# Two edits to the attention of a fused sequence layer: an addition made by a product with the identity, and one pair moved behind the first convolution

## The chip, the cores and the metric

The kernel runs on one core of a Trainium2 chip. The core has TensorE (PE: matrix products from SBUF into PSUM), VectorE (DVE), ScalarE (ACT), GpSimd (POOL) and SyncE (SP), each with its own instruction stream; they meet through semaphores. TensorE's loading of weights appears in the profile as a row of its own (PEld). All data are fp32. The metric is the device time of one execution in microseconds (us); lower is better. Before the change it is 3857.62 us, the median of three runs (3856.37 to 3858.19).

## The reference

x has 4 batches, 512 time steps, 128 frequencies and 64 channels, so D = 8192 numbers a time step. Layer 0 computes, for each batch:

```
xn = layernorm(x)                          # over D
k, v, r = xn @ Wk, xn @ Wv, sigmoid(xn @ Wr)   # 64 numbers a step
s_t = decay * s_(t-1) + k_t * v_t          # a scan over time
x = x + (r * s) @ Wo                       # the attention
x = x + gelu(conv over frequency(layernorm(x)) + freq_b)
x = x + layernorm(depthwise conv over time(layernorm(x)) + time_b)
x = x + gelu(x @ W1 + b1) @ W2 + b2        # on the 64 channels
```

Layer 1 takes a moving average over time, and adds what a Fourier transform, a product for each channel, and the inverse transform make of the rest. The change touches only the attention and the convolution over frequency of layer 0.

## The kernel before

Layer 0 keeps time on the free axis: D is cut into 64 chunks of 128 rows, taken as 32 pairs of chunks, and a tile of a pair has 128 partitions and 2 x 512 numbers. Each batch goes through five stages: `project` (J) and `scan` (Z), `attend_and_convolve` (A), `convolve_time` (C), `open_feed` (O) and `feed_forward` (F). Two stages of different batches run side by side. `in_turn` steps two Python generators in turn, by the share that each `yield` states: batch 0's A beside batch 1's J; then batch 0's C beside batch 1's A; then batch 0's F beside batch 2's J, batch 1's C beside batch 2's A, batch 1's F beside batch 3's J, batch 2's C beside batch 3's A, and so on. A lead given for each stretch sets how far one side runs ahead.

The order of TensorE's instructions is the order in which these generators issue them. The other engines are ordered by the framework's scheduler, which also sets the semaphores; each engine then works its own list strictly in order. Transfers into SBUF are issued on SP's queue, stores on POOL's.

The stage that the change touches is A, from L466. For pair i it has three steps:

- `attend(i)`, L475: SP loads x of the pair (`xp`, three buffers) and a 128x128 piece of Wo (`wo_sb`). TensorE makes two products with 64 rows each (L482) into the PSUM tile `a`, which has two banks and one buffer, so a product waits until the one before has been read. VectorE adds x (L484), which gives `x1` in SBUF, and multiplies by the layer norm's factor of each time step (L488), which gives `z`.
- `convolve(i)`, L498: three groups of products, L503 (the norm's mean and the bias), L512 (the neighbouring chunks: pairs i-1 and i+1) and L517 (the chunk itself), into the tile `c` or `m`. ScalarE applies GELU in place (L518), VectorE adds `x1` (L520), which gives `x2`; POOL stores it, ScalarE squares it (L523), and scales the weights of pair i+2 (L496).
- `add_up(i)`, L250: TensorE sums x2 and its square over the rows into the tile `st`, for the next layer norm.

The loop at L533 issues `attend(i)`, `convolve(i - 2)`, `add_up(i - 3)`. The first convolution therefore follows the third `attend`, though it needs only pairs 0 and 1.

In C each pair costs VectorE two operations on 128x1024 (L556, L557) and four on 128x512 (L564), and ScalarE two activations (L560) and a square (L605); its column sums on TensorE go to the tile `p`. Batch 0's C makes all 32 pairs there; for batches 1 and 2, 12 of the 32 pairs have been made during an earlier F (`AHEAD`). When A begins, C's layer norm is not ready: its first step is the `finish` of the A before it (L262, L240), which stands on TensorE behind the first three convolutions of the A beside it.

Of the kernel before, what the change touches and what calls it, by code (L numbers as in the profile page):

```python
# [10 lines left out]
F32 = mybir.dt.float32  # L11
AF = mybir.ActivationFunctionType
ALU = mybir.AluOpType
# [3 lines left out]
P = 128  # L17
# [5 lines left out]
SL = 512  # L23
NS = D // SL
NPR = NCH // 2
# [54 lines left out]
def layer0(ctx, tc, dram, x, xt, vecs, wkvr, wo, wdec, wconv, fbias, w1, fb1, w2, fb2, x4):  # L80
# [4 lines left out]
    nc = tc.nc  # L85
# [7 lines left out]
    fr = ctx.enter_context(tc.tile_pool(name="fr", bufs=3))  # L93
# [9 lines left out]
    def two(pool, tag):  # L103
        return pool.tile([P, 2, SL], F32, tag=tag, name=tag)


    ident = const.tile([P, P], F32, name="ident")
# [51 lines left out]
    def neighbours(q, c):  # L159

        return (c - 1, q), (c + 1, 1 - q)

    def rows_of(q, d):

        return 1 - q if d < 0 else q
# [79 lines left out]
    def add_up(st, i, pair, squares, first, last):  # L245

        for j in range(2):
            for k, src in ((0, pair), (1, squares)):
                q = 2 * j + k
                nc.tensor.matmul(  # L250
                    st[32 * q : 32 * q + 32, :], lhsT=ones, rhs=src[:, j, :],
                    start=first, stop=last,
                )

    def finish(st, bank, tag):

        s_sb = rowp.tile([P, SL], F32, tag="s", name="s_sb")
        nc.scalar.copy(s_sb, st)
        yield CHAIN
        pm = bank()  # L260
        for t in range(NT):
            nc.tensor.matmul(  # L262
                pm[:, 2 * t : 2 * t + 2], lhsT=s_sb[:, t * P : (t + 1) * P], rhs=pick,
                start=True, stop=True,
            )
        me = tiny.tile([P, NT, 2], F32, tag=f"me{tag}", name="me")
        nc.vector.tensor_copy(me.rearrange("p t k -> p (t k)"), pm[:, 0 : 2 * NT])
        return me[:, :, 0], me[:, :, 1]

    def moments(mean, square, tag):  # L270

        var, rs, mrs = cols(f"var{tag}"), cols(f"rs{tag}"), cols(f"mrs{tag}")
        nc.vector.tensor_tensor(var, mean, mean, ALU.mult)
        nc.vector.tensor_tensor(var, square, var, ALU.subtract)
        rsqrt(rs, var)
        nc.vector.tensor_tensor(mrs, mean, rs, ALU.mult)
        return rs, mrs

    def rows(bank, a, b, names):
        both = rowp.tile([P, 2, SL], F32, tag=names, name=names)  # L280
        for k, col in enumerate((a, b)):
            pb = bank()
            spread(pb, col)
            nc.scalar.copy(both[:, k, :], pb)
            yield CHAIN
        return both[:, 0, :], both[:, 1, :]

    def pair_of(row):
        return row.unsqueeze(1).to_broadcast([P, 2, SL])

    def load_x(b, i):
        xp = fr.tile([P, 2, SL], F32, tag="xp", name="xp")
        nc.sync.dma_start(xp, xt[b, 2 * i : 2 * i + 2].rearrange("c p t -> p c t"))
        return xp
# [4 lines left out]
    def c_bank():  # L299
        return two(ps_c, "c")  # L300
# [165 lines left out]
    def attend_and_convolve(b):  # L466
        rst, rs, mrs = scanned.pop(b)
        rb, mb = yield from rows(of_a, rs, mrs, "rm")

        nc.vector.tensor_scalar(mb, mb, at_one[:, 1:2], at_one[:, 0:1], ALU.mult, ALU.add)  # L470
        st = ps_s.tile([P, SL], F32, tag="s", name="st")
        free_s[0] = False
        x1s, zs, ws, waiting = {}, {}, {}, {}

        def attend(i):  # L475
            xp = load_x(b, i)
            wo_sb = fr.tile([P, P], F32, tag="wo", name="wo_sb")
            nc.sync.dma_start(wo_sb, wo[:, i, :])
            at = two(ps_a, "a")
            for j in range(2):  # L480
                js = slice(j * S, (j + 1) * S)
                nc.tensor.matmul(at[:, j, :], lhsT=wo_sb[js, :], rhs=rst[js, :], start=True, stop=True)  # L482
            x1 = x1s[i] = fr.tile([P, 2, SL], F32, tag="x1", name="x1")
            nc.vector.tensor_tensor(x1, at, xp, ALU.add)  # L484
            z = fr.tile([P, 2, SL], F32, tag="z", name="z", bufs=4)
            for j in range(2):
                zs[2 * i + j] = z[:, j, :]
            nc.vector.tensor_tensor(z, x1, pair_of(rb), ALU.mult)  # L488

        def scaled(i):  # L490

            wcs = fr.tile([P, 2, P + H], F32, tag="wcs", name="wcs")
            for j in range(2):
                c = 2 * i + j
                ws[c] = wcs[:, j, :]
                nc.scalar.mul(wcs[:, j, :], wc_sb[:, i % 2, :], vec[:, G2, c : c + 1])  # L496

        def convolve(i):  # L498
            cv = c_bank() if i % 2 or held[0] else two(ps_m, "m")
            for h in range(2):  # L500
                for j in range(2):
                    q = 32 * (2 * h + j)
                    nc.tensor.matmul(  # L503
                        cv[h * H : (h + 1) * H, j, :], lhsT=cgr[q : q + 2, i, :], rhs=mb[q : q + 2, :],
                        start=True, stop=False,
                    )
            for j in range(2):
                c = 2 * i + j
                for n, h in neighbours(i % 2, c):
                    if 0 <= n < NCH:  # L510
                        rs = halves[rows_of(n // 2 % 2, n - c)]
                        nc.tensor.matmul(  # L512
                            cv[halves[h], j, :], lhsT=ws[n][rs, P:], rhs=zs[n][rs, :], start=False, stop=False
                        )
            for j in range(2):
                c = 2 * i + j
                nc.tensor.matmul(cv[:, j, :], lhsT=ws[c][:, 0:P], rhs=zs[c], start=False, stop=True)  # L517
            nc.scalar.activation(cv, cv, AF.Gelu_apprx_tanh)  # L518
            x2 = two(bk, "x2")
            nc.vector.tensor_tensor(x2, cv, x1s.pop(i), ALU.add)  # L520
            nc.gpsimd.dma_start(x2d[b][2 * i : 2 * i + 2].rearrange("c p t -> p c t"), x2)
            sq2 = bk.tile([P, 2, SL], F32, tag="sq", name="sq2")
            nc.scalar.activation(sq2, x2, AF.Square)  # L523
            for c in (2 * i - 2, 2 * i - 1):
                zs.pop(c, None)
                ws.pop(c, None)
            if i + 2 < NPR:
                scaled(i + 2)
            waiting[i] = x2, sq2

        for i in range(2):
            scaled(i)
        for i in range(NPR + 3):  # L533
            if i < NPR:
                attend(i)
                yield 1.0
            if 1 < i < NPR + 2:
                convolve(i - 2)
                yield 5.0
            if i > 2:  # L540
                add_up(st, i - 3, *waiting.pop(i - 3), i == 3, i == NPR + 2)
                yield 1.0
        begin[attend_and_convolve], free_s[0] = b + 1, True
        mean3, sq3 = yield from finish(st, of_a, 3)
        carried[b] = moments(mean3, sq3, 3)
# [206 lines left out]
    def nothing(b):  # L752
        yield 1.0

    J, Z, A, C, O, F = project, scan, attend_and_convolve, convolve_time, open_feed, feed_forward
    begin[A] = 0
    needed = {A: scanned, C: carried, O: causal, F: opened}
# [317 lines left out]
```

## Time and profile before

| what | value |
|---|---|
| median of the runs | 3857.62 us |
| the profiled execution's own time | 3842.84 us |
| its span, first to last instruction | 3840.8 us |
| TensorE busy | 3619.7 us, 94% |
| VectorE busy | 2692.2 us, 70% |
| ScalarE busy | 1764.0 us, 46% |
| GpSimd busy | 504.2 us, 13% |
| mean granted clock of TensorE | 0.984 |
| L484, x1 = a + x | 128 times, 1219 ns |
| L488, z = x1 times the factor | 128 times, 1219 ns |
| first `wo` product of batches 0, 1, 2, 3 | 219.95, 510.49, 1250.37, 1939.74 us |
| last column sum into `st` of batches 1, 2 | 790.9, 1491.1 us |

A line of the trace in order of time has the start, the duration (both in us), engine, line of the kernel, operation, what it writes and reads with its shape, the number of instructions merged into it, and in brackets how long the engine was idle before it and whom it waited for. Matmuls are pipelined and their ends are modelled, so that TensorE's duration and busy time run ahead of what it gets done; the distance from start to start is the better measure. VectorE's instructions overlap by some 0.1 us as well.

### The profile page before, as it was taken

The page shows a single profiled execution, that of the slowest core. Times are in us where ns is not written, and L with a number is a line of the kernel's source. Part 1 is how long each engine was busy: PE and PEld are TensorE (multiplying, and loading weights), DVE is VectorE, ACT ScalarE, POOL GpSimd, SP SyncE. Part 2 cuts the span into 40 slices and gives each one's busy share as a digit, 9 for nine tenths or more (in the row PEclk, how much of TensorE's full clock was granted, in tenths as well). Part 3 has the DMA queues.
Part 4 walks back from the last instruction along what each step waited for, and adds up shares of the span by engine and source line. Part 5 has one row for each costly group of instructions (what it writes and reads, how often), then busy time and mean ns, then how long its engine had stood idle before and what let it go on. Part 6 is the DMA issues. An engine that isn't in the chain of part 4 may idle for free. (4 is left out here: it accounts for less than half of the span.)

```text
span 3840.8 us, 44890 instructions
## 1 busy us (share of the span) xinstructions
PE 3619.7 (94%) x15945; PEld 1342.6 (35%) x15945; DVE 2692.2 (70%) x3498; ACT 1764.0 (46%) x2491; POOL 504.2 (13%) x782
## 2 busy tenths in 40 slices
PE   9999999988999999899999989999989999999999
PEld 4433322233333223333322323333322753327533
DVE  4455669968656896865689799855559267893577
ACT  0023345645556564555656578867744210142100
POOL 0000012212000121110022121100012100121001
PEclk9999999999999999999999999999999999999999
DMA  9867657777765788777568677645559468994687
GB/s 312 273 216 244 222 195 253 257 246 272 256 227 185 234 276 265 252 255 235 193 232 277 215 243 260 219 154 175 186 190 284 141 212 293 306 311 160 197 292 269
DMA packets 428599, 910.71 MB, mean 237 GB/s; under 512 B 33688, under 2 KB 84056, under 8 KB 424280
## 3 DMA queue, kind: packets, MB, share of 16 engines
q1 hardware_dynamic: 350080, 634.55, 50.3%
q0 software_dynamic: 75776, 271.62, 20.1%
q8 instruction: 127, 2.08, 0.2%
q10 hardware_dynamic: 2520, 1.67, 0.2%
q14 instruction: 96, 0.79, 0.1%
HBM read 639.21 MB, written 268.50 MB: 236 GB/s over the span
## 5 line engine op out<-in xcount | busy, mean ns | idle before, releaser
L667 PE MATMUL pa<-mid,w_sb 128*64 128x512 f32 x2048 | 503.7, 613 | 70.1 <-DVE x4t L672 69.9
L660 ACT ACTIVATE mid<-m,fb_sb 128x1024 f32<-128x1024 f32 x256 | 284.7, 1112 | 243.4 <-PE m L656 243.0
L672 DVE SCALAR_TENSOR_TENSOR x4t<-pa,fb_sb,x 128x512 f32<-128x512 f32 x252 | 187.6, 745 | 208.2 <-PE pa L667 208.2
L656 PE MATMUL m<-x,w_sb 64*128 64x512 f32 x1008 | 291.6, 651 | 1.0 <-ACT mid L660 0.7
L660 ACT ACTIVATE mid<-c,fb_sb 128x1024 f32<-128x1024 f32 x256 | 283.2, 1106 | 1.6 <-PE c L656 1.6
L667 PEld LDWEIGHTS pa<-mid,w_sb 128*64 128x64 f32 x2048 | 125.8, 137 | 417.5 <-issue 221.1
L656 PE MATMUL c<-x,w_sb 64*128 64x512 f32 x1008 | 265.6, 600 | 5.0 <-ACT mid L660 4.9
L360 PE MATMUL a<-xp,wx 128*128 128x512 f32 x512 | 245.0, 605 | 6.2 <-DVE wx L357 5.5
L943 PE MATMUL b<-xin,avg_sb 128*128 128x512 f32 x512 | 230.8, 593 | 3.1 <-DVE xin L949 3.1
L920 ACT COPY two<-a 128x512 f32<-128x512 f32 x64 | 37.5, 586 | 423.9 <-PE a L915 423.9
L523 ACT ACTIVATE sq<-x 128x1024 f32<-128x1024 f32 x128 | 135.0, 1054 | 203.0 <-DVE x L520 203.0
L949 DVE TENSOR_TENSOR xin<-b,pm 128x512 f32<-128x512 f32 x256 | 159.0, 683 | 95.5 <-PE b L946 80.5
L564 DVE SCALAR_TENSOR_TENSOR to<-kd,vec,to 128x510 f32<-128x510 f32 (+1 forms) x288 | 210.5, 743 | 17.9 <-ACT to L560 16.2
L633 ACT ACTIVATE kd<-kd,vec 128x512 f32<-128x512 f32 x256 | 193.5, 809 | 7.2 <-DVE kd L625 7.2
L250 PE MATMUL st<-x,ones 128*32 128x512 f32 x512 | 174.3, 603 | 14.0 <-DVE x L520 13.8
L825 DVE COPY xf<-b 128x256 f32<-128x256 f32 x128 | 54.3, 424 | 188.4 <-PE b L889 187.8
L681 PEld LDWEIGHTS pt<-ident,x4t 128*128 128x128 f32 x1024 | 107.9, 141 | 210.3 <-ACT mid L660 155.0
L846 DVE TENSOR_TENSOR uv<-xin 128x1024 f32<-128x1024 f32 x128 | 155.2, 1228 | 35.2 <-DMA edge<-x 14.7
L344 DVE BATCH_NORM_STATS2 stt<-wx 128x6 f32<-128x512 f32 x174 | 113.0, 685 | 93.3 <-DMA wx<-in_x 92.8
L357 DVE TENSOR_SCALAR wx<-wx,vec 128x192 f32<-128x192 f32 x174 | 48.6, 316 | 184.7 <-DMA wx<-in_wkvr 167.6
L482 PE MATMUL a<-rst,wo_sb 64*128 64x512 f32 x512 | 147.6, 650 | 32.3 <-DVE x L484 30.0
L484 DVE TENSOR_TENSOR x<-a,xp 128x1024 f32<-128x1024 f32 x128 | 156.0, 1219 | 20.9 <-PE a L482 17.6
(239 smaller groups left out, 6649.0 us busy)
## 6 DMA issues: line engine op xcount, KB each, us to landing
xp<-in_xt SPq DMA_DIRECT2D x256, 512.0 KB
xin<-x SPq DMA_DIRECT2D x128, 1024.0 KB
kh<-to SPq DMA_DIRECT2D x152, 512.0 KB
x<-x POOLq DMA_DIRECT2D x128, 512.0 KB, 4.1
kx<-x SPq DMA_DIRECT2D x128, 512.0 KB
x<-ob POOLq DMA_DIRECT2D x64, 1024.0 KB, 6.6
out<-xin POOLq DMA_DIRECT2D x64, 1024.0 KB, 7.3
x<-x SPq DMA_DIRECT2D x96, 512.0 KB
```

Source lines behind the costliest of these rows:

```text
L250: nc.tensor.matmul(st[32 * q : 32 * q + 32, :], lhsT=ones, rhs=src[:, j, :], start=first, stop=last,)
L360: nc.tensor.matmul(pa[:, k, :], lhsT=wq[:, j, k * P : (k + 1) * P], rhs=xp[:, j, :], start=first and j == 0, stop=last and j == 1,)
L484: nc.vector.tensor_tensor(x1, at, xp, ALU.add)
L564: nc.vector.scalar_tensor_tensor(to[:, j, k:], xr[:, j, : SL - k], vec[:, w, c], to[:, j, k:], ALU.mult, ALU.add)
L633: tc.keep_in_program_order(nc.scalar.activation(d[:, j, :], d[:, j, :], AF.Identity, bias=vec[:, B4, c], scale=vec[:, G4, c]))
L656: nc.tensor.matmul(pm[:, h, :], lhsT=w1_sb[hs, m * P : (m + 1) * P], rhs=x3[hs, :], start=True, stop=True)
L660: nc.scalar.activation(mid, pm, AF.Gelu_apprx_tanh, bias=fb1_sb[:, m : m + 1])
L667: nc.tensor.matmul(pa[h * H : (h + 1) * H, :], lhsT=w2_sb[:, m, :], rhs=mid[:, h, :], start=(m == 0), stop=(m == 1),)
L672: nc.vector.scalar_tensor_tensor(x4t, pa, fb2_sb, x3s[c // 2][:, c % 2, :], ALU.add, ALU.add)
L846: nc.vector.tensor_tensor(t, xin[:, 0:2, :], xin[:, 2:4, :], op)
L943: nc.tensor.matmul(po[j], lhsT=avg_sb[:, j, :], rhs=xin[:, j, :], start=True, stop=False)
L949: nc.vector.tensor_tensor(by_n(xin[:, j, :]), by_n(po[j]), by_c(pm[j % 2][:, j // 2, :]), ALU.add)
```

## The change

Two edits, both in `attend_and_convolve`. In batch 1, for the odd pairs, TensorE adds x: behind the two products with Wo it makes two more into the same PSUM tile, with the identity as weights and `xp` as the moving operand. ScalarE then copies the sum to `x1`, and VectorE makes `z` from the PSUM tile, not from `x1`. In all four batches the third pair's `attend` is issued behind the first convolution, with its two loads, and the step that it had in the taking of turns is left out.

```diff
             at = two(ps_a, "a")
+
+            summed = b == 1 and i % 2 == 1
             for j in range(2):
                 js = slice(j * S, (j + 1) * S)
-                nc.tensor.matmul(at[:, j, :], lhsT=wo_sb[js, :], rhs=rst[js, :], start=True, stop=True)
-            x1 = x1s[i] = fr.tile([P, 2, SL], F32, tag="x1", name="x1")
-            nc.vector.tensor_tensor(x1, at, xp, ALU.add)
+                nc.tensor.matmul(at[:, j, :], lhsT=wo_sb[js, :], rhs=rst[js, :], start=True, stop=not summed)
+            base = x1 = x1s[i] = fr.tile([P, 2, SL], F32, tag="x1", name="x1")
+            if summed:
+                for j in range(2):
+                    nc.tensor.matmul(at[:, j, :], lhsT=ident, rhs=xp[:, j, :], start=False, stop=True)
+                nc.scalar.copy(x1, at)
+                base = at
+            else:
+                nc.vector.tensor_tensor(x1, at, xp, ALU.add)
             z = fr.tile([P, 2, SL], F32, tag="z", name="z", bufs=4)
             for j in range(2):
                 zs[2 * i + j] = z[:, j, :]
-            nc.vector.tensor_tensor(z, x1, pair_of(rb), ALU.mult)
+            nc.vector.tensor_tensor(z, base, pair_of(rb), ALU.mult)
...
         for i in range(NPR + 3):
-            if i < NPR:
+            if i < NPR and i != 2:
                 attend(i)
                 yield 1.0
             if 1 < i < NPR + 2:
                 convolve(i - 2)
+                if i == 2:
+
+                    attend(i)
                 yield 5.0
```

## The prediction

> **What bounds the kernel now.** I read, in this order, the page's slices, sums over stretches, and VectorE's and TensorE's instructions in order of time.
>
> The slices first: TensorE is at 8 or 9 tenths everywhere, so most of the kernel hangs on it; VectorE reaches 9 in only a few slices (96 us each).
>
> ```profile
> PE   9999999988999999899999989999989999999999
> ...
> DVE  4455669968656896865689799855559267893577
> ```
>
> Slices 6 to 8 are batch 1's attention beside batch 0's time convolution (first `wo` product 510.49 us, last sum 790.9). The sums by engine (TensorE, its weight loads, VectorE, ScalarE, GpSimd, then clock, DMA share, GB/s) for that stage and for batch 2's attention beside batch 1's time convolution:
>
> ```profile
> 1272.00:1491.00 219.00, 213.00 (x1215) 55.28 (x1214) 185.96 (x185) 135.08 (x186) 45.95 (x65) 1.00 0.78 259
> 545.00:786.00 241.00, 222.01 (x1119) 51.98 (x1118) 240.48 (x263) 148.45 (x202) 67.86 (x88) 1.00 0.78 260
> ```
>
> In batch 1's stage VectorE is busy 240.48 of 241 us: it is the bound, and ScalarE has 92 us free. In batch 2's stage 12 of the 32 pairs of the time convolution were made earlier, VectorE has 33 us free and TensorE leads. In batch 1's stage VectorE runs like this:
>
> ```profile
> 742.23 1.22 DVE L556 TENSOR_TENSOR kd<-x,rm 128x1024 f32<-128x1024 f32 x1
> 743.36 1.22 DVE L484 TENSOR_TENSOR x<-a,xp 128x1024 f32<-128x1024 f32 x1
> 744.49 0.74 DVE L564 SCALAR_TENSOR_TENSOR to<-kd,vec,to 128x511 f32<-128x511 f32 x1
> 745.15 1.22 DVE L488 TENSOR_TENSOR z<-x,rm 128x1024 f32<-128x1024 f32 x1
> 746.29 1.40 DVE L564 SCALAR_TENSOR_TENSOR to<-kd,vec,to 128x510 f32<-128x510 f32 x2
> ```
>
> Starts lie 1.13 to 1.14 us apart behind a 128x1024 operation and 0.66 behind an L564. A pair of attention costs three of the former (L484, L488, L520), 3.42; a pair of the time convolution two and four L564, 4.92. TensorE is the one that waits:
>
> ```profile
> 753.60 1.13 PE L482 MATMUL a<-rst,wo_sb 64*128 64x512 f32 x4 [0.78 <-DVE x L484]
> 754.66 1.09 PE L503 MATMUL m<-rm,cgr 2*64 2x512 f32 x8
> 755.68 1.09 PE L512 MATMUL m<-z,wcs 64*64 64x512 f32 x8
> 756.70 1.98 PE L517 MATMUL m<-z,wcs 128*128 128x512 f32 x4
> ```
>
> By starts, L482 takes 1.06, L503 1.02, L512 1.02 and L517 1.91; the column sums take 0.99 (st) and 0.93 (p). The start of the stage is another matter:
>
> ```profile
> 512.94 1.13 PE L482 MATMUL a<-rst,wo_sb 64*128 64x512 f32 x4 [1.32 <-DVE x L484]
> 515.40 1.13 PE L482 MATMUL a<-rst,wo_sb 64*128 64x512 f32 x4 [1.32 <-DVE x L484]
> 516.46 1.09 PE L503 MATMUL m<-rm,cgr 2*64 2x512 f32 x8
> 517.47 1.65 PE L512 MATMUL m<-z,wcs 64*64 64x512 f32 x6
> 519.06 3.06 PE L517 MATMUL m<-z,wcs 128*128 128x512 f32 x4
> 522.05 1.13 PE L482 MATMUL a<-rst,wo_sb 64*128 64x512 f32 x4
> ```
>
> Tile a has one buffer, so each `wo` product waits for VectorE's read of the one before. After these waits L517 takes 2.99 instead of 1.91: the granted clock is 0.64 at 517 to 520 us, and 0.50 at 1948 to 1952, behind the same waits of batch 3's attention.
>
> **What the Trainium skill says.** "TensorE: Matmul & The Clock Gate", section What's actually happening: an idle window of about 3.4 us halves TensorE's clock. The trace agrees: 0.50, and L503 1.91 instead of 1.02. "PSUM — Partial Sum Buffer", section PSUM bank collisions raise a hardware error: two engines may not be in one bank's quadrant at once, two reads by ScalarE and VectorE included, so schedulers order them. Before never reads a with two engines; in the changed program z's instruction of each summed pair waits for ScalarE, the copy ahead of it. "VectorE: DVE Perf Modes", section The TRN2 errata: an fp32 tensor_tensor takes (N+151)/0.96 ns, 1224 for 1024 elements; the rows have 1219 for L484 (one input in PSUM) and L488 (none), so reading a instead of x1 costs z nothing. The same section's ScalarE row gives (172+1024)/1.2 = 997 ns for the new copy, an estimate; the GELU of that shape in PSUM takes 1002 in the trace. I take 1.0.
>
> **The change, part by part.** All in the profiled execution's time, 3842.84 us (span 3840.8). The median of the runs is 14.8 us above; I carry the difference over unchanged.
>
> *Batch 1, steady part.* Removed on VectorE: L484 of the odd pairs. The stage is full from about 538 us, pair 5 on, so 14 of the 16 count: 14 x 1.14 = 16.0 us. Added on TensorE: two 128x128 by 512 fp32 products per odd pair, the form of L517, 1.91 a pair. From pair 6's product (545.19) to 790.9 us TensorE's sum by starts is now 26 x 1.06 + 28 x 3.95 + 28 x 0.99 + 32 x 0.93 = 195.7 in 245.7 us; 13 odd pairs add 24.8, making 220.5. So 50 us of slack shrink to 25 as VectorE's load shrinks to some 230, and TensorE stands at 96% of it. What a nearly full TensorE loses, batch 2's stage tells: its sum is 28 x 1.06 + 30 x 3.95 + 30 x 0.99 + 32 x 0.93 = 207.7 in 219 us, 5.4% over. With that loss 220.5 becomes 232.5, a gain of 13; VectorE without any loss gives 16. As both limits hold at once and pairs of the time convolution come unevenly, I take a gain of 11, with 5 and 16 as ends.
>
> Hidden: 14 copies, 14 us, in ScalarE's 92 free. z stands behind the copy, and VectorE's next work (L520, then the taps) behind z. In the changed order a copy stands behind the Square of pair i-3, hence behind its L520, and between that L520 and z VectorE has four taps and an L556, 3.8 us; Square, one activation and copy take 1.05 + 0.8 + 1.0 = 2.9. So the copy comes 0.9 early. If that cover goes, each us is paid 14 times.
>
> *Batch 1, start.* New order on TensorE: products 0 and 1, first convolution, products 2 and 3, second convolution. Pair 1 gets 1.91 of identity product, then copy 1.1 and z 1.3 before L512 can start: 512.94 + 1.06 + 1.91 + 2.4 = 518.3 (now 517.47); the convolution ends at 521.2. Product 2 follows at once, but VectorE's order has the first L520 ahead of product 2's sum: GELU 1.1, L520 1.3, sum 1.3 after 521.2, so product 3 waits until 524.9, ends with its identity product at 527.9, and the second convolution at 531.8, where it is 527.06 now. That is 4.7 later; now 1.9 of half clock is inside, and I assume a similar loss again in part: +5.5 (4 to 7). The time convolution's first spread stands on TensorE behind the third convolution, so VectorE's full stretch starts later by as much.
>
> *Batches 2 and 3, start.* Same order without identity products. Batch 2: L512 needs pair 1's z, ready at 1259.9 (two instructions of the time convolution come between); convolution to 1262.8, product 3 after 1.1 + 1.3 + 1.3 at 1266.5, second convolution to 1271.5 at full clock, against 1271.33 now with 3.6 of half clock inside. TensorE would be idle 4.2 and 2.7 us, so half clock again: +2.5 (0 to 4). Batch 3 likewise: 1959.8 at full clock against 1960.68, so +2 (-1 to 3.5). TensorE leads these stages, so it is paid in full. Batch 0: products for batch 1's projection (L360) fill both gaps: 0.
>
> *Moved transfers.* Pair 2's xp and wo loads go with it on SP's queue; no convolution issues there, batch 1's projection loads do in batch 0. xp has three buffers and is asked for a pair or two ahead: 0. On GpSimd's queue nothing moves but the first x2 store, with its L520.
>
> Sum: -11 + 5.5 + 2.5 + 2 + 0 = -1.0 us: 3841.8 profiled, 3856.6 for the median. No change within 0.2% (7.7 us, about what a measurement can tell).
>
> **Rivals.** *Faster:* the steady loss is small (gain 15) and the clock is kept at the starts (+4, +0.5, +0.5): -10, 3847.6. For it: VectorE's time convolution work needs no TensorE and filled every gap so far. Against: TensorE's slack of 50 us made that possible. *Slower:* z behind the copy stalls VectorE. At 1.0 us in 14 pairs the gain of 11 turns into 3 lost, in all +13, 3870.6. It decides from 0.6 us a pair. For it: ScalarE waits 40 us on L564 and GpSimd before its Squares in this stage, and the copy stands behind them. Against: the 0.9 of cover. *The relief isn't felt:* the queue of loads waits 108 us for L556 in this stage, so x2 might be late once VectorE is quicker; gain about 0, in all +10, 3867.6. Against: VectorE never waited for DMA there, DMA is at 78%.
>
> **Numbers.** Forecast 0.54, faster 0.22, stall behind the copy 0.18, late loads 0.06. So faster 0.22, same 0.54, slower 0.24. The range reaches to the faster rival and the stalled one, 3847 to 3870; the forecast's own is 3851 to 3864.
>
> **What would show it.** L484 gone from 16 pairs and 16 ScalarE copies of about 1.0 us; batch 1's last sum 4 to 7 us earlier than 790.9; VectorE below 98% there with short waits for the copy; products 3 of batches 1 to 3 waiting about 2.7 us; second convolutions 2 us late in batches 2 and 3. Wrong if z waits more than 0.6 us per odd pair, or if the starts lose nothing.

## The result, and the profile after

The changed kernel is slower: 3883.45 us median (3862.52 to 3891.7) against 3853.12 us of the kernel before, ten executions each. The medians lie 30 us apart; the ratio of the two kernels, which is used from here on, is 1.0067, 95% interval 1.0051 to 1.0084, some 26 us. Forecast was no change. The profiled execution took 3883.17 us (span 3881.4), that of before 3842.84; before's is one of its quicker executions, so stages, not spans, are compared below. In the changed kernel the lines are renumbered: L482 is L484, L484 is L492, L488 is L496, L520 is L528, L555 is L566, L556 and L557 are L567 and L568, L560 is L571, L564 is L575; the identity product is L488, the copy L489.

The slices of the page, changed kernel (TensorE, VectorE, TensorE's granted clock):

```profile
PE   9999999998999999899989988899989999999999
...
DVE  4445649978756796775579799945549267892577
...
PEclk9999989999999999999989999999999999999999
```

Slice 6 (numbered from 1, 485 to 582 us) is where batch 0's attention ends and batch 1's begins; its clock is down to 8. The same two stretches as in the prediction, set off from each batch's own start (TensorE, its weight loads, VectorE, ScalarE, GpSimd, clock, DMA share, GB/s):

```profile
561.00:802.00 241.00, 229.83 (x1172) 62.30 (x1170) 228.95 (x245) 159.99 (x212) 63.33 (x85) 0.95 0.77 258
1301.00:1519.40 218.40, 216.29 (x1227) 57.12 (x1226) 185.89 (x186) 136.38 (x188) 46.28 (x65) 0.99 0.76 260
```

In batch 1's stage VectorE is busy 95% instead of 99.8%, TensorE 95% instead of 92%, at a clock of 0.95 instead of 1.00. VectorE was relieved, and the stage is not shorter. Where the time went, by stage:

| from, to | before | changed | difference |
|---|---|---|---|
| batch 0's first `wo` product to batch 1's first | 290.5 | 305.8 | +15.3 |
| batch 1's first to its last column sum | 280.4 | 290.8 | +10.4 |
| batch 2's, same | 240.7 | 240.2 | -0.5 |
| batch 3's, same | 242.8 | 251.4 | +8.6 |

The column of before is at the low end: in the profiles of the experiments below, those whose edit leaves the stage alone take 289.7 to 299.7 us in the first row and 282.4 to 284.5 in the second. Of the +15.3 and the +10.4 some 6 us each are therefore clear of scatter. Batch 0 still has a loss, to which the forecast gave nothing; batch 1 has lost where a gain was forecast; batch 3 has lost more than said and batch 2 nothing.

### The profile page after: what moved, and what is told of

Read it like the earlier page. It is cut to its first block, busy times and chain, and to the rows that moved or that the text cites. A ratio compares the mean times of both kernels' runs of the same rounds, so it can differ in the third digit from the quotient of the medians.

```text
span 3881.4 us, 44990 instructions
## 1 busy us (share of the span) xinstructions
PE 3665.1 (94%) x16009; PEld 1358.0 (35%) x16009; DVE 2682.0 (69%) x3482; ACT 1780.9 (46%) x2507; POOL 503.6 (13%) x782
## 3 DMA queue, kind: packets, MB, share of 16 engines
q1 hardware_dynamic: 350080, 634.55, 48.9%
## 5 line engine op out<-in xcount | busy, mean ns | idle before, releaser
L671 ACT ACTIVATE mid<-m,fb_sb 128x1024 f32<-128x1024 f32 x256 | 284.5, 1111 | 247.2 <-PE m L667 246.9
L575 DVE SCALAR_TENSOR_TENSOR to<-kd,vec,to 128x511 f32<-128x511 f32 (+1 forms) x288 | 212.1, 746 | 22.8 <-ACT to L571 20.0
L357 DVE TENSOR_SCALAR wx<-wx,vec 128x192 f32<-128x192 f32 x174 | 48.5, 317 | 204.8 <-DMA wx<-in_wkvr 192.1
L857 DVE TENSOR_TENSOR uv<-xin 128x1024 f32<-128x1024 f32 x128 | 156.0, 1229 | 37.8 <-PE a L866 17.1
L484 PE MATMUL a<-rst,wo_sb 64*128 64x512 f32 x512 | 150.4, 665 | 31.4 <-DVE x L492 21.2
L529 POOL DMA_DIRECT2D x<-x x128 | 93.3, 729 | 640.8 <-DVE x L528 636.5
L692 PE MATMUL pt<-ident,x4t 128*128 128x128 f32 x1024 | 169.6, 289 | 1.5 <-ACT ob L699 1.5
```

The costliest lines, as they stand in the source:

```text
L575: nc.vector.scalar_tensor_tensor(to[:, j, k:], xr[:, j, : SL - k], vec[:, w, c], to[:, j, k:], ALU.mult, ALU.add)
L671: nc.scalar.activation(mid, pm, AF.Gelu_apprx_tanh, bias=fb1_sb[:, m : m + 1])
L692: nc.tensor.transpose(pt[:, t, :], x4t[:, t * P : (t + 1) * P], ident)
L857: nc.vector.tensor_tensor(t, xin[:, 0:2, :], xin[:, 2:4, :], op)
```

## Experiments: which part of the change costs

All single kernels below are compared with the kernel before, run on the same chip: ratio and interval, and the microseconds that the ratio makes of 3855. The table gives, from one profiled execution each, stretches from the start of one pair's z to that of another's. A profiled execution lies up to 15 us from the median of its kernel. Where a stage is untouched by the edit it scatters: batch 0 from 208.9 to 214.8, the start of batch 1 from 38.7 to 42.8, batches 2 and 3 by about 3 and 1 us. "Products only" adds x twice in batch 1's odd pairs, and "relief only" leaves x out there; they serve for timing alone.

| kernel | ratio | us | batch 0, pairs 0 to 24 | batch 1, 0 to 6 | batch 1, 6 to 31 | batch 2, 0 to 31 | batch 3, 0 to 31 |
|---|---|---|---|---|---|---|---|
| before | 1 | 0 | 210.7 | 38.7 | 220.5 | 218.8 | 221.0 |
| changed | 1.0067 | +26 | 218.8 | 50.4 | 220.2 | 219.0 | 229.7 |
| identity only | 1.0009 | +3.5 | 211.5 | 50.9 | 221.8 | 217.3 | 220.7 |
| move only | 1.0063 | +24 | 224.0 | 46.5 | 217.9 | 222.8 | 229.2 |
| move, batch 0 | 1.0027 | +10 | 220.9 | 40.3 | 220.5 | 220.1 | 221.9 |
| move, batches 1-3 | 1.0033 | +13 | 210.8 | 48.9 | 217.9 | 217.6 | 229.4 |
| move, turn kept | 1.0040 | +15 | 213.6 | 47.7 | 220.5 | 226.0 | 226.0 |
| move in batch 0, x2 loads on GpSimd | 1.0008 | +3 | 213.1 | 42.8 | 220.4 | 220.0 | 221.1 |
| identity from pair 7 on | 0.9990 | -4 | 208.9 | 42.7 | 221.5 | 217.2 | 221.1 |
| products only | 1.0065 | +25 | 209.7 | 43.6 | 232.5 | 217.9 | 220.8 |
| relief only | 0.9997 | -1 | 214.0 | 43.5 | 216.0 | 218.5 | 221.5 |
| relief only, new order of taps | 0.9986 | -5 | 210.0 | 45.5 | 210.7 | 218.6 | 220.7 |
| changed, new order of taps | 1.0051 | +20 | 215.3 | 49.1 | 216.3 | 219.5 | 229.0 |

**The two parts apart.** The first is the changed kernel with the third pair at its old place:

```
-            if i < NPR and i != 2:
+            if i < NPR:
                 attend(i)
...
-                if i == 2:
-                    attend(i)
```

> Only the identity products, ScalarE copies and z from a in batch 1's odd pairs; the third pair stays where it was. The prediction's sums give -11 for the steady part and about +2 at the start (one identity pair and one copy ahead of the first convolution), so about -9 us against before (ratio 0.998). Theory A (the loss sits in the moved pair of batch 0, through the queue of loads) says the same, -5 to -10 us. Theory B (what VectorE saves is eaten by a TensorE that is nearly full, waits for z and falls to half clock) says 0 to +10 us, with the granted clock of batch 1's stage at 0.95 to 0.97 instead of 1.00.

Measured: 1.0009 (1.0000 to 1.0017). The second keeps the move and sets `summed = False`:

> Only the moved third pair, in all four batches; no identity products. The prediction's sums give +5 to +8 us (starts of batches 1 to 3). Theory A says +16 in batch 0's stage and +4 each in some of batches 1 to 3, +18 to +28 us in all, as much as the whole change. Theory B gives the move only the starts, +5 to +10 us, and most of the rest to the identity products.

Measured: 1.0063 (1.0040 to 1.0085). The next two do the move with `i == 2 and b == 0`, and with `i == 2 and b > 0`:

> Only the moved third pair, and in batch 0 alone. The prediction said 0. Theory A says +10 to +16 us, with the seventh pair of batch 0's attention about 6 us and the tenth about 9 us later than before, VectorE waiting longer for batch 1's projection loads. Theory B says 0.

Measured: 1.0027 (1.0014 to 1.0040).

> Only the moved third pair, in batches 1 to 3. The prediction's sums give +5 to +8 us. Theory A: 0 to +8 us, since TensorE's later work in batch 2 made the start up again and only batch 3's may stay. If this one is +15 or more, the loss is in the starts and not in the loads of batch 0.

Measured: 1.0033 (1.0021 to 1.0046). The parts add up within their intervals: 10 + 13 make the move's 24, and 24 + 3.5 the whole 26. The move is nine tenths of the loss, and two fifths of the move are paid in batch 0. The identity products neither gain the 11 of the forecast nor lose much. The stages of the table agree: with the turn dropped and the loads left on SyncE's queue, batch 0 takes 215.3 to 224.0 us in every kernel that moves its pair, and batch 3 is late by 8 us in every kernel that moves its own (by 5 with the turn kept).

## Experiments: batch 0

SyncE's waits for the store of x2 from 215 to 300 us (us in total, times, longest), before and then changed:

```profile
SPq L555 <- DMA x<-x: 6.8, 1, 6.8
```

```profile
SPq L566 <- DMA x<-x: 18.0, 3, 8.5
```

The waiting instruction is the load of x2 for batch 0's time convolution, far ahead of its use. It waits for the store of x2, and every load behind it waits too. In all four kernels that move batch 0's pair, drop the turn and leave these loads on SyncE, it waits 16.6 to 18.0 us, in three pieces; where batch 0 is left alone, 4.3 to 7.6, nearly always in one. The queue in order of time, before:

```profile
238.51 0.51 SPq L337 DMA_DIRECT2D wx<-in_wkvr  x1
...
240.41 0.56 SPq L555 DMA_DIRECT2D x<-x  x1
```

and changed:

```profile
242.15 0.37 SPq L566 DMA_DIRECT2D x<-x  x1
243.77 0.37 SPq L337 DMA_DIRECT2D wx<-in_wkvr  x1
...
253.19 0.37 SPq L566 DMA_DIRECT2D x<-x  x1
...
255.70 0.46 SPq L337 DMA_DIRECT2D wx<-in_wkvr  x1
```

Before, the load of batch 1's projection weights (L337) is issued ahead of the x2 load; changed, it stands behind it. The first convolution and its x2 come earlier in the program now, so the scheduler lists their loads earlier. Counted from batch 0's first product, the sixth L337 is issued at 60.5 us before, at 60.4 to 63.7 in the other kernels that leave batch 0 alone (61.4 with the identity edit), at 69.1 in the changed kernel, and at 71.0 and 72.4 with the move in all batches and in batch 0 alone. VectorE needs those weights for L357, and TensorE's list has the products of both stages in one fixed order, so the attention becomes late with the projection. Two ways to undo it were tried. The first leaves the move in batch 0 and takes three loads off SyncE's queue:

```
-        nc.sync.dma_start(x2, x2d[b][...])
+        q = nc.gpsimd if b == 0 and i < 3 else nc.sync
+        q.dma_start(x2, x2d[b][...])
```

> The third pair moved in batch 0 alone, as in the run with the move in batch 0, and the first three loads of x2 for batch 0's time convolution issued by GpSimd instead of SyncE. In the moved order these three stand on SyncE's queue ahead of batch 1's projection loads and wait there 16.6 us for the stores of x2 (6.8 before). If that wait is what makes batch 0's stage late: back to within 4 us of before, and 8 to 12 us faster than the move in batch 0. If it is the order of the products on TensorE or the lost turn: as late as the move in batch 0, +10.

Measured: 1.0008 (0.9997 to 1.0019), where the move in batch 0 had 1.0027; the sixth L337 is issued at 63.9. The same edit to the kernel before is the control:

> The kernel before with the same three loads on GpSimd's queue: what that costs or gives by itself. Before waits 6.8 us there, once, and another load stands in front of it: 0 to -4 us.

Measured: 1.0003 (0.9993 to 1.0012), nothing. The second way asks why the lists changed. The diff drops a `yield 1.0` with the pair, so that the attention (A) has one step less in the taking of turns and the projection's step comes later beside it. It is put back:

```
                 if i == 2:
                     attend(i)
+                    yield 1.0
                 yield 5.0
```

> The third pair moved in all four batches, no identity products, but the turn that the change drops (the share 1.0 behind the third pair) is kept, behind the moved pair. The loads of batch 1's projection then stand on SyncE's queue ahead of the x2 loads as they do before, except the first. If the dropped turn makes batch 0's loss: 6 to 12 us faster than the move with the turn dropped (+24 us against before), so +12 to +18. If the place of the product itself makes it: the same +24.

Measured: 1.0040 (1.0026 to 1.0054), 9 us better than with the turn dropped, though the two intervals overlap (1.0040 to 1.0085 there). The waits of SyncE in this kernel:

```profile
SPq L566 <- DMA x<-x: 7.8, 1, 7.8
```

One wait again, as before; batch 0 takes 213.6 us to pair 24. So the missed cost in batch 0 is shown by two repairs that each bring the stage back into the scatter: it is the x2 loads ahead of the projection's loads, put there by the dropped turn. Moving the product by itself costs batch 0 nothing that stands out of the scatter.

## Experiments: the starts of batches 1 to 3

With the turn kept, batches 2 and 3 lose 7 and 5 us at the start and keep that to the end: pair 4's z stands 28.3 and 26.7 us behind pair 0's, where before it is 21.0 and 21.8, and the totals are 226.0 and 226.0. With the turn dropped, batch 2 loses 2 to 7 at the start and its stage makes it up in three of four kernels, and batch 3 loses 3 more on the way in all four. Why these two stages differ there was not tried. TensorE at the start of batch 3, changed kernel:

```profile
1985.38 1.53 PE L484 MATMUL a<-rst,wo_sb 64*128 64x512 f32 x4 [2.11 <-DVE x L492]
1986.84 1.98 PE L511 MATMUL c<-rm,cgr 2*64 2x512 f32 x8
...
1990.66 3.03 PE L525 MATMUL c<-z,wcs 128*128 128x512 f32 x4
```

Product 3 waits as forecast (2.11 us; 2.7 was said). The cost that was too small is the clock: L511 takes 1.91 by starts instead of 1.02, and nearly the whole second convolution passes at half speed, as the first did. In the records of the clock, batch 3's attention has 20 us at half clock in the changed kernel, where it had 10.2 before.

Batch 1's start with the identity edit alone, engines mixed:

```profile
524.96 2.67 PE L488 MATMUL a<-xp,ident 128*128 128x512 f32 x4
527.72 1.01 ACT L489 COPY x<-a 128x1024 f32<-128x1024 f32 x1 [7.27 <-PE a L488]
528.76 1.23 DVE L496 TENSOR_TENSOR z<-a,rm 128x1024 f32<-128x1024 f32 x1 [4.60 <-ACT x L489]
530.04 2.08 PE L484 MATMUL a<-rst,wo_sb 64*128 64x512 f32 x4 [2.40 <-DVE z L496]
...
535.87 3.78 PE L525 MATMUL m<-z,wcs 128*128 128x512 f32 x4
```

The tile `a` is now free only when copy and z have both ended, 2.4 us behind the identity product instead of the 1.3 that a sum takes. TensorE waits that long and then runs at half clock from 530 to 540 us, and the first convolution ends 19.1 us behind the first product, where before it was 11.6. How much half clock falls on this start differs between executions, and in the eight kernels whose edit leaves it alone (before among them) the scatter goes with it: 38.7 us with 3.4 us of half clock, 40.3 with 6.8, 42.6 to 42.8 with 13.7. The move and the identity products do not add up there (46.5 and 48.9 for the move, 50.9 for the products, 50.4 for both): in the changed kernel product 2 stands behind the convolution and no longer waits for z. There the half clock falls on products 1 and 3 with their identity products, and both convolutions pass at full clock:

```profile
542.12 2.08 PE L484 MATMUL a<-rst,wo_sb 64*128 64x512 f32 x4 [2.43 <-DVE x L492]
544.13 2.67 PE L488 MATMUL a<-xp,ident 128*128 128x512 f32 x4
546.73 1.09 PE L511 MATMUL c<-rm,cgr 2*64 2x512 f32 x8
```

If the start is most of the loss of the identity edit, leaving it out must give it back:

```
-            summed = b == 1 and i % 2 == 1
+            summed = b == 1 and i % 2 == 1 and i > 6
```

> Identity products, copies and z from a only in batch 1's odd pairs from 7 on (13 of 16), third pair not moved. In the identity edit alone, batch 1's seventh pair stood 12 us later than before and the last pair another 0 to 1. If the loss is all in the start, and the steady part neither gains nor loses, this kernel is 0 to 3 us from before, and 4 to 10 us faster than the identity edit in all odd pairs in the same stage. The prediction's steady gain of 11 would show here undisturbed: -10 us against before. If instead TensorE loses in the steady part what VectorE saves and more, it is +2 to +6.

Measured: 0.9990 (0.9979 to 1.0002), 7 us better than all odd pairs; the start is 42.7. So the steady part, 221.5, stays within 1.1 us of before with 13 sums taken off VectorE.

## Experiments: why the relief of VectorE gives nothing

The prediction's own rival was z behind ScalarE's copy. Here z comes first, and the copy behind it:

```
             if summed:
                 ...
-                nc.scalar.copy(x1, at)
                 base = at
...
             nc.vector.tensor_tensor(z, base, pair_of(rb), ALU.mult)
+            if summed:
+                nc.scalar.copy(x1, at)
```

> The identity edit alone, with z made straight from a and ScalarE's copy behind it, so that z waits for no copy; a is held until the copy has ended. If z behind the copy were the loss (the rival of the prediction): 6 to 12 us faster than the identity edit alone. If the loss is TensorE's load and its half clock: within 3 us of it.

Measured: 1.0029 (1.0016 to 1.0041), not better but worse. In the changed kernel's stage (526 to 817 us) the waits of z for the copy and of TensorE for z are

```profile
DVE z L496 <- ACT x L489: 11.7, 3, 4.6
...
PE a L484 <- DVE z L496: 8.3, 6, 2.4
```

three of 16, those of pairs 1, 3 and 5, all ahead of the steady part; behind pair 6 no z waits for its copy. As the loss of the steady part, that rival is out. Next, the two halves of the edit: the identity products without the relief, and the relief without the products.

```
                 for j in range(2):
                     nc.tensor.matmul(at[:, j, :], lhsT=ident, rhs=xp[:, j, :], start=False, stop=True)
-                nc.scalar.copy(x1, at)
-                base = at
-            else:
-                nc.vector.tensor_tensor(x1, at, xp, ALU.add)
+            nc.vector.tensor_tensor(x1, at, xp, ALU.add)
```

> The identity products alone: VectorE's sum stays in every pair (so x is added twice in batch 1's odd pairs) and there is no copy. TensorE carries 16 x 1.91 us more and VectorE as much as before. The prediction's view (TensorE has 50 us of slack in the steady part) gives +5 us, from the start alone. If TensorE's load costs in the steady part too: +12 to +25 us, with a lower granted clock there.

Measured: 1.0065 (1.0044 to 1.0086).

```
             if summed:
-                for j in range(2):
-                    nc.tensor.matmul(at[:, j, :], lhsT=ident, rhs=xp[:, j, :], start=False, stop=True)
                 nc.scalar.copy(x1, at)
                 base = at
```

> The relief alone: in batch 1's odd pairs VectorE's sum is replaced by the copy on ScalarE and z is made from a, but there are no identity products (x is not added in those pairs). If VectorE bounds the stage, as the prediction read it: -12 to -16 us against before. If relief of VectorE isn't felt there at all (late loads, or another bound): -3 to +3.

Measured: 0.9997 (0.9986 to 1.0007). Both surprise: 32 us of products cost 25 in a stage where TensorE had 50 us of slack by its sum, and 18 us of VectorE's work (16 sums at 1.14), gone from an engine that is 99.8% busy, give nothing that the total shows and 4.5 in the steady part (216.0 instead of 220.5). Of the 25 us the steady part shows 12 (232.5 instead of 220.5); the first-to-last time of the stage, 296.3 us, is 12 to 16 above those of untouched stages, and the rest was not located.

A first theory was the hold of `a`, the time from a product to the last read of its tile. With the relief only, the 12 odd pairs hold it 9.13 us, and the next product follows within 0.2 us in 11 of them; before, all pairs hold it 8.51 (odd and even pairs of relief only together hold it 7.8, which speaks against the theory already). So z was made from the copy in SBUF (the line `base = at` left out), which frees `a` as soon as ScalarE is done: in the relief alone, in the identity edit from pair 7 on, and in all odd pairs.

> Relief alone as before (no sum on VectorE and no identity products in batch 1's odd pairs, so x is not added there), but z is made from ScalarE's copy in SBUF, so that a is free when the copy ends. If the hold of a by z took the relief: -8 to -14 us against before, and the hold in odd pairs falls from 9.1 to some 3 us. If another limit lies behind VectorE: within 3 us of before, as with z from a.

> Identity products and copies in batch 1's odd pairs from 7 on, z made from the copy; third pair not moved. If the hold of a by z took the relief: -7 to -12 us against before, 4 to 8 us faster than with z from a (-4). If TensorE's load took it: -2 to -5, the same as with z from a.

> The identity edit in all odd pairs of batch 1, z made from the copy; third pair not moved. With z from a it was +3.5 us. If the hold of a is the cause, 5 to 12 us faster than that, so -9 to -2 against before; the start still pays for its three identity pairs, some 6 us. If TensorE's load is the cause: +1 to +5.

Measured: 0.9986 (0.9977 to 0.9996), 0.9991 (0.9981 to 1.0001) and 1.0009 (1.0000 to 1.0017), each within 5 us of its twin with z from `a`; pairs 6 to 31 take 216.2, 220.8 and 221.5. The hold in the odd pairs did not fall to 3 us either, but to 8.4 to 8.7: the copy stands in ScalarE's list behind a square (L523 of before) that waits for VectorE's x2, so VectorE's pace comes back through it. The theory falls. The start is 43.2 in the third of these where the identity edit had 50.9, but the totals are the same 1.0009, and the two profiled executions had 3.4 and 17.1 us of half clock there, so no gain at the start is shown.

These twins settle another rival. TensorE has 20.5 us of half clock between pairs 6 and 31 of the changed kernel and none before; is that what takes the relief? Relief only, z from `a` and then z from the copy, pairs 6 to 31:

```profile
565.25:781.25 216.00, 195.05 (x1008) 49.03 (x1008) 211.41 (x229) 144.52 (x194) 61.77 (x80) 0.93 0.78 267
567.28:783.50 216.22, 201.34 (x1031) 47.81 (x1030) 211.57 (x229) 144.19 (x194) 62.21 (x80) 0.99 0.78 267
```

The clock is 0.93 in one and 0.99 in the other (30.7 and 3.4 us at half), and the time is the same; the identity edit and its twin likewise take 221.8 at 0.96 and 221.5 at 0.99. Half clock does not set the time of this stretch.

What does take the relief shows in VectorE's own instructions, changed kernel (the taps are the `scalar_tensor_tensor` instructions of the time convolution, L564 before, two for each half of a pair):

```profile
703.30 1.23 DVE L567 TENSOR_TENSOR kd<-x,rm 128x1024 f32<-128x1024 f32 x1
704.56 1.22 DVE L568 TENSOR_TENSOR kd<-kd,rm 128x1024 f32<-128x1024 f32 x1
705.71 1.22 DVE L528 TENSOR_TENSOR x<-m,x 128x1024 f32<-128x1024 f32 x1
706.84 1.52 DVE L575 SCALAR_TENSOR_TENSOR to<-kd,vec,to 128x511 f32<-128x511 f32 x2
708.75 1.53 DVE L575 SCALAR_TENSOR_TENSOR to<-kd,vec,to 128x511 f32<-128x511 f32 x2 [0.38 <-ACT to L571]
```

L568 reads what L567 has just written, and starts 1.26 us behind it; L528 reads something else and starts 1.15 behind L568. Two taps of one half, the second of which reads the first's result, take 1.53 us; two that are apart take 1.41. The last line also waits 0.38 us for ScalarE's activation of the other half (L571). In the program's order, from pair 6's z to the last one, a first tap is followed directly by a second tap 5 times before (3 times by the one that reads it), and 35 times in the changed kernel (30 times). By starts, over those pairs, with the lines of before:

| VectorE, us | before | changed | relief only | same, new order | changed, new order | products only |
|---|---|---|---|---|---|---|
| sums, L484 (25; 12 where relieved) | 28.4 | 13.6 | 13.6 | 14.4 | 14.6 | 28.4 |
| taps (107 to 111) | 71.8 | 83.3 | 80.2 | 73.6 | 78.4 | 81.1 |
| one tap | 0.67 | 0.75 | 0.74 | 0.68 | 0.71 | 0.74 |
| L556 and L557 (56 or 57) | 63.6 | 66.6 | 65.4 | 65.9 | 66.6 | 66.3 |
| z and L520 | 56.7 | 56.7 | 56.8 | 56.8 | 56.7 | 56.7 |
| second tap directly behind the first that it reads, times | 3 | 30 | 25 | 0 | 0 | 28 |
| L557 directly behind its L556, times | 0 | 14 | 14 | 16 | 14 | 12 |
| L556 directly behind a tap that it waits for, times | 7 | 19 | 15 | 13 | 22 | 12 |
| idle for ScalarE's L560 | 0 | 3.3 | 2.7 | 0 | 2.3 | 3.5 |

The 14.8 us that the sums leave in the changed kernel are eaten by taps (+11.5) and by L556 and L557 (+3.0). Of this, 3.8 are work of the time convolution that now falls between these pairs (four taps and one L556), 6.3 are instructions directly behind the one they wait for (27 taps, 14 L557 and 12 L556 more, 0.12 us each), and 4.1 are delays of first taps that wait for ScalarE.

Products only is in the table because it answers the surprise above. It keeps every sum, and still its list has 28 such pairs of taps:

```profile
690.83 1.53 DVE L569 SCALAR_TENSOR_TENSOR to<-kd,vec,to 128x511 f32<-128x511 f32 x2
692.74 1.54 DVE L569 SCALAR_TENSOR_TENSOR to<-kd,vec,to 128x511 f32<-128x511 f32 x2 [0.39 <-ACT to L565]
```

So it is not the missing sums alone that bring the pairs together: the scheduler lists VectorE's work otherwise as soon as the products are added. VectorE is busy 227.2 of the 232.5 us in that kernel, and taps (+9.3) and L556 with L557 (+2.7) make up the 12 us; 2.5 of it are two taps and one L556 more between these pairs. Its list, with the waits for ScalarE in it, accounts for the steady loss; what the products' load on TensorE costs by itself in this stretch was not separated, for products only was not run with the taps in another order.

To test the part of the taps, those of batch 0's time convolution were put into an order in which none stands right behind the one it reads from, and the scheduler was told to keep it:

```
-            for k, w in ((1, W1), (2, W0)):
+            for k, w in ((1, W1), (2, W0)) if b else ():
                 nc.vector.scalar_tensor_tensor(
...
+        for k, w in () if b else ((1, W1), (2, W0)):
+            for j in range(2):
+                c = slice(2 * i + j, 2 * i + j + 1)
+                tc.keep_in_program_order(nc.vector.scalar_tensor_tensor(
+                    to[:, j, k:], xr[:, j, : SL - k], ...
```

> Relief alone, z from a (no sum on VectorE and no identity products in batch 1's odd pairs, x not added there), and the taps of batch 0's time convolution in the order first tap of both halves, then second tap of both. If instructions behind the one they read from took the relief: taps at 0.66 us from start to start, batch 1's pairs 6 to 31 in 205 to 210 us instead of 216, -7 to -14 us against before. If not: as without the new order, -1 to -3.

Measured: 0.9986 (0.9975 to 0.9998); pairs 6 to 31 take 210.7 us instead of 216.0, and a tap 0.68 instead of 0.74. VectorE in that kernel:

```profile
704.94 1.22 DVE L563 TENSOR_TENSOR kd<-kd,rm 128x1024 f32<-128x1024 f32 x1
706.08 1.22 DVE L526 TENSOR_TENSOR x<-m,x 128x1024 f32<-128x1024 f32 x1
707.21 2.73 DVE L576 SCALAR_TENSOR_TENSOR to<-kd,vec,to 128x511 f32<-128x511 f32 x4
709.86 1.22 DVE L494 TENSOR_TENSOR z<-a,rm 128x1024 f32<-128x1024 f32 x1
```

Four taps in 2.73 us, where the changed kernel takes 1.53 for two and waits 0.38 us before the next two.

> The kernel before with the new order of the taps in batch 0's time convolution. Its taps already start 0.66 us apart, since sums stand between them: -2 to +2 us.

Measured: 1.0010 (0.9998 to 1.0023): by itself the order gives nothing, 222.0 in that stretch.

> Identity products and copies in batch 1's odd pairs from 7 on, z from the copy, third pair not moved, and the new order of the taps. Without it: -3.5 us. If the suspicion holds: -6 to -12; TensorE's load keeps it from the full 14. If not: -2 to -5.

Measured: 0.9990 (0.9978 to 1.0001), steady part 215.9 instead of 220.8.

> The changed kernel with the new order of the taps. The changed kernel is +26 us. If the suspicion holds, 4 to 8 us less, +18 to +22; if TensorE alone sets the pace of its steady part, +24 to +28.

Measured: 1.0051 (1.0037 to 1.0064), steady part 216.3 instead of 220.2. So in three kernels that have lost sums the new order takes 4 to 5 us off this stretch, and in the one that has not it takes none. The stretches show it; the totals move the same way by 0 to 6 us, and their intervals overlap, so for the whole time it is not shown. The order also takes away waits for ScalarE (2.7 us to none in relief only, 3.3 to 2.3 in the changed kernel), so what it gives is not the close pairs alone: 25 of them at 0.12 us make 3 of the 5.3 us in relief only, while in the changed kernel 30 of them make 3.6 of 3.9. With the new order the identity products still cost 5 to 6 (216.3 and 215.9 against 210.7).

Left after all this: every version that adds x once and does not move the pair is ahead of the changed kernel without doubt (0.9990 to 1.0029 against 1.0067); against the kernel before, the best of them, 0.9990, is no gain that was measured.

## Why the prediction was wrong, by its own steps

**Batch 0, "0", and "Moved transfers", "0": the main failure.** They were to cost nothing and cost 10 us (the move in batch 0 alone). The prediction looked at the loads that go with the pair, and said of the x2 store only that it moves; it did not go on to the x2 loads that follow that store and wait on SyncE's queue in front of another stage's loads. Nor did it price the `yield` that the diff drops with the pair, of which the run with the turn kept gives some 9 us back. The trace of before shows that wait, once, 6.8 us.

**Starts of batches 2 and 3, +2.5 and +2.** The mechanism was right: product 3 waited 2.5 and 2.1 us, for the sum behind L528. The size was off: 7 and 5 us with the turn kept, where the clock is halved for 20 and 17 us, through both convolutions, instead of 10.2 in each batch, through one. In the changed kernel batch 2 starts 4 us late and gives this back, and batch 3 starts 5 late and loses 8.7.

**Start of batch 1, +5.5.** Measured 11.7 against the profile of before, 8 to 12 over all executions with an untouched start. Product 3 waited 2.43 us. At the prediction's own mark, the end of the second convolution, the loss is 7.9. The order of events was right; what was too small is the clock, but not at the convolutions: products 1 and 3 with their identity products took 4.52 and 4.61 us by starts instead of 2.97, 3.2 us of half clock where 0.8 was put. Behind that mark comes pair 5's identity product, 1.9 us, which stands in neither of the prediction's sums: the steady part counts the products from pair 7 on.

**Steady part of batch 1, -11.** Measured -0.3. The step that failed is the price of a removed sum, 1.14 us, its distance from start to start. Removed alone, twelve sums gave 4.5 us instead of 13.7, because the rest of VectorE's list then stands behind its own instructions (5.4 us) and waits for ScalarE (3.3). The prediction took VectorE's list as fixed but for the sums, and the scheduler made another one. TensorE's slack of 50 us as cover for the identity products was not borne out either: they cost 12 us (232.5) without the relief and 4 to 6 with it. Without the relief VectorE's list accounts for that; with it the split is open. That products only took the 232.5 us which the prediction had for a full TensorE is chance as far as the profiles show: VectorE was busy 98% of it, TensorE 93%.

**Rivals.** Slower by z behind the copy: the kernel is slower, but not by this. Its mark, more than 0.6 us of waiting per odd pair, is met in the mean (11.7 us over 16 pairs), yet all of it lies in pairs 1, 3 and 5, and putting z first made the kernel no faster. Relief not felt: came true in its effect, and not by late x2 loads, as VectorE waited for no DMA in this stage. The range ended at 3870, 13 us below the median.

**What would show it.** The 16 copies of 1.0 us are there (992 ns), and VectorE is below 98% (95%), though its gaps in the steady part are late starts behind VectorE's own instructions and 3.3 us of waits for L571, not waits for the copy. Batch 1's last column sum is 26 us later instead of 4 to 7 earlier.

The Trainium skill, "TensorE: Matmul & The Clock Gate", section What's actually happening, was used with an idle window of about 3.4 us. Here waits of 2.1 to 2.4 us were followed by half clock, in stretches where TensorE had idled shortly before as well, and around these starts the clock's records show half clock in pieces of 3.4, 6.8 or 10.2 us. The measured stretches decide, and the starts had to be priced with more half clock than the forecast took.

## What to carry to other kernels

A step that is moved takes along what follows from it: list the loads that wait for its stores, and what stands behind them on the same queue. An engine at 99.8% is a bound only at the pace that its order allows: before pricing a removed instruction at its distance from start to start, look at which instructions come to stand next to each other, and whether the second reads the first. And where a scheduler makes the lists, an edit to one engine's work can change another engine's list: products only left VectorE's instructions as they were, and VectorE took 12 us longer for them.

## What was not expected of the hardware

- On VectorE a 128x1024 tensor_tensor right behind the one it reads from started 1.26 us behind it, 1.13 to 1.14 otherwise; a pair of dependent taps took 1.53 us instead of 1.41 (starts 0.78 apart instead of 0.66).
- Executions of the changed kernel lie 29 us apart (3862.52 to 3891.7), those of before 20, and the profiled executions differ in where TensorE's clock is halved: a wait of some 2 us was followed by about 10 us at half clock in one (530 to 540 us of the identity edit, clock 0.50).
- Half clock cost nothing where VectorE led (216.0 us with 30.7 us of it, 216.2 with 3.4), and time went with it at the start of batch 1, where TensorE waits and leads (38.7 us with 3.4, 42.6 to 42.8 with 13.7).
